# A table's copies moved to ScalarE and its zeros to GpSimd; in a chain of two pairs, ScalarE in program order and the pairs one turn apart

## The chip, the cores and the metric

The kernel runs on one core of one Trainium2 chip. The time is device microseconds (us) of one execution; lower is better. A core has five instruction queues that run beside each other: TensorE (PE, with its weight loads shown as PEld), VectorE (DVE), ScalarE (ACT), GpSimd (POOL) and SyncE (SP), which issues most of the DMAs. ScalarE and GpSimd issue some DMAs too. Instructions of different queues wait for each other through semaphores.

## The reference, cut to what matters

Four layers follow each other on an activation `x` of 4 batches x 512 tokens x 128 channels, all float32. Each layer is a half-weighted feed-forward part, an attention-like part, and the same feed-forward part again. The parts that this change touches are these:

```python
# layer 0: a mixture of 8 experts (top 1), then attention with a relative-position table
x = x + 0.5 * L0_ffn(layernorm(x), ...)            # "first mixture"
x = x + L0_attn(layernorm(x), ..., rel_pos_emb)    # the table: 16 heads, causal
...
# the end of layer 1, layer 2, and the start of layer 3
x = x + 0.5 * L1_ffn(layernorm(x), ...)   # sigmoid scores, top 2 of 8, swiglu experts, a shared one
x = x + 0.5 * L2_ffn(layernorm(x), ...)   # top 2 of 8 by logits; y += gate_e * (x @ w_in_e.T @ w_out_e.T)
x = x + L2_attn(layernorm(x), ...)        # sigmoid gates, then h = 0.9 h + 0.1 g over the tokens
x = x + 0.5 * L2_ffn(layernorm(x), ...)
x = x + 0.5 * L3_ffn(layernorm(x), ...)   # "third mixture": top 2 of 8 experts with a capacity
```

The relative-position table of layer 0 is `rel_pos_emb` summed over the 8 channels of a head, and it enters the attention scores as a bias that depends on the distance of the two tokens.

## The kernel before, in words

A batch of 512 tokens is a tile `xs[b]` of 128 partitions x 4 token blocks x 128 channels, and it stays in SBUF from the first to the last part. The kernel is written with a planner that decides the order of each queue at compile time: among the instructions that it takes to be ready it prefers those that stand earlier in the program. Inside `tc.manual_schedule(engines={...})` the named queues keep the order of the program instead.

**The table.** `prep_table` (L1012 and on) builds the bias table, 128 partitions x 16 heads x 512. A short row for each head is written to DRAM (`tab_rows`). Eight DMAs on ScalarE's queue (L1037), for two heads each, read it back so that each partition is shifted by one (`rev`, 128x512). TensorE turns each block over with the matrix `flip` into a PSUM bank (L1042), VectorE copies the bank into the last 256 columns of the table (L1043), and VectorE sets the other 256 columns of all heads to zero (L1044). This generator is run out at the end of a block in which all four compute queues keep the order of the program, after the routing of the first mixture (`f00.tokens`) and ahead of its experts (`f00.experts`). The same block ends with the transposed biases `b1T` (L570, a VectorE copy at L571) and with zeros that GpSimd writes for the attention (`padded_values`, L585). The experts themselves are not in the block, so the planner may put their instructions between those of the block. Per expert TensorE transposes the tokens (L466), multiplies with `w1` (L490), ScalarE and VectorE evict with the bias `b1T` (L494, L495), TensorE multiplies with `w2` (L526), and GpSimd scatters the rows to DRAM (L512). `rev` comes out of the pool tag `"raw"` of five buffers, which the zeros `z` of the mixture and `b1r` use as well.

**The chain.** From the second feed-forward part of layer 1 to the routing of the third mixture the batches go in two pairs, `[0, 1]` and `[2, 3]`, each a generator `behind(pool, bs)`. It runs `l1_ffn`, `l2_ffn`, `l2_attn`, `l2_ffn` and `f30.tokens`. A `yield` ends a step, and `skewed(gens, lag)` runs one step of each pair per turn, pair 0 ahead, with pair 1 starting `lag` turns later. What a pair does in its steps, counted from 0 in each part:

- `l1_ffn`: 12 steps for pair 0, whose norms and gates were made during the attention; 17 for pair 1, which first makes norms (`norms`, L168 to L187: VectorE statistics, GpSimd `rstd` and `off`, then half of the tiles on ScalarE at L182 and half on VectorE at L186), transposes (L195, copies at L1124), scores and gates. The gates go to DRAM and come back spread over partitions (`cb`, L1242). For each of five chunks: two matmuls (L1218, L1219), a sigmoid (L1222), two VectorE products (L1223, L1224), a GpSimd product with `cb` (L1265), and the down matmuls (L1253).
- `l2_ffn`: 9 steps. Steps 0 to 2 are norms and transposes, 3 the logits (L1133) and the first products (L1419), 4 the routing on VectorE and two sigmoids (L1434, L1436), 5 to 8 are the four gated rounds: 16 VectorE instructions each (L1450) that add a gated product to `x`.
- `l2_attn`: 9 steps: 3 of norms, then for each batch projection and two sigmoids (L1471, L1473), the scan over the tokens on VectorE (L1478), and the output.
- `f30.tokens`: norms (all on ScalarE), logits, the exponential (L348), routing on VectorE, and 16 scatters per pair by GpSimd's indirect DMA (L416). Pair 0 takes two steps of it per turn and one scatter per step.

In this stage GpSimd keeps the order of the program; the other queues are ordered by the planner. Before it stands the attention of layer 1, behind it the experts of the third mixture, whose first load waits for the last scatter.

Of the kernel before, what the change touches and what calls it, by code (L numbers as in the profile page):

```python
# [9 lines left out]
FP = mybir.dt.float32  # L10
# [7 lines left out]
P = 128  # L18
D = 128
NB, S = 4, 512  # L20
# [4 lines left out]
NH = 16  # L25
# [16 lines left out]
def kernel(ctx: ExitStack, tc: tile.TileContext, a: dict, out: bass.AP):  # L42
    nc = tc.nc
# [5 lines left out]
    stage = ctx.enter_context(tc.tile_pool(name="stage", bufs=5))  # L49
# [3 lines left out]
    def const(shape, name, dtype=FP):  # L53
        return cpool.tile(shape, dtype, name=name, tag=name)

    def bank(name):
        return psum.tile([P, 512], FP, name=name, tag="bank", bufs=8)
# [19 lines left out]
    flip = const([P, P], "flip")  # L77
# [934 lines left out]
    def prep_table(pool):  # L1012


        rel = stage.tile([P, D], FP, name="rel", tag="rel", bufs=1)
        nc.sync.dma_start(rel, a["L0_attn_rel_pos_emb"][P - 1 : 2 * P - 1, :])
        yield

        table = pool.tile([P, NH, S], FP, name="table", tag="table", bufs=1)
        tab = stage.tile([P, NH], FP, name="tab", tag="tab", bufs=1)  # L1020
        nc.vector.tensor_reduce(tab, rel.rearrange("p (h d) -> p h d", d=HD), AX.X, ALU.add)
        ps = bank("tabT")
        nc.tensor.matmul(ps[:NH, :P], tab, flip, start=True, stop=True)
        last = stage.tile([NH, 1], FP, name="tab_last", tag="tab_last", bufs=1)
        nc.vector.tensor_copy(last, ps[:NH, 0:1])
        row = stage.tile([NH, 3 * P], FP, name="tab_row", tag="tab_row", bufs=1)
        nc.vector.memset(row[:, :P], 0.0)
        nc.vector.tensor_scalar(row[:, P : 2 * P], ps[:NH, :P], last, None, ALU.subtract)
        nc.vector.memset(row[:, 2 * P :], NEG)
        rows = dram.tile([NH, 3 * P], FP, name="tab_rows", tag="tab_rows")  # L1030
        nc.sync.dma_start(rows, row)
        yield

        for h in range(0, NH, 2):

            rev = stage.tile([P, 2, 2 * P], FP, name=f"rev{h}", tag="raw")
            nc.scalar.dma_start(  # L1037
                rev,
                bass.AP(tensor=rows.tensor, offset=rows.offset + h * 3 * P, ap=[[1, P], [3 * P, 2], [1, 2 * P]]),
            )  # L1040
            ps = bank(f"turned{h}")
            nc.tensor.matmul(ps, flip, rev.rearrange("p h s -> p (h s)"), start=True, stop=True)  # L1042
            nc.vector.tensor_copy(table[:, h : h + 2, S - 2 * P :], ps.rearrange("p (h s) -> p h s", h=2))  # L1043
        nc.vector.memset(table[:, :, : S - 2 * P], 0.0)  # L1044
        l0["table"] = table
        yield

# [523 lines left out]
    def whole(parts):  # L1571
        for _ in parts:
            pass

    def skewed(gens, lag):

        live = {i: g for i, g in enumerate(gens)}
        r = 0
        while live:
            for i in list(live):  # L1580
                if r >= i * lag and next(live[i], "end") == "end":
                    del live[i]
            r += 1
            yield
# [19 lines left out]
    pairs = [[b, b + 1] for b in range(0, NB, 2)]  # L1604
    gate0T = wpool.tile([D, E], FP, name="gate0T", tag="gate0T")
    ps = bank("gate0T")
    nc.tensor.transpose(ps[:, :E], gate0, ident[:E, :E])
    nc.vector.tensor_copy(gate0T, ps[:, :E])
    with tc.tile_pool(name="tables", bufs=1) as tables:
        f00 = Mixture("f00", CAP0, 1)  # L1610
        f00.zeroed(stage, "raw", 5)
        made = prep_table(tables)
        next(made)
        whole(f00.empty())
# [31 lines left out]
    with tc.tile_pool(name="weights12", bufs=1) as mid:  # L1646
# [39 lines left out]
        def behind(pool, bs):  # L1686
            yield from l1_ffn(pool, 1, bs, early if bs[0] == 0 else None)
            yield from l2_ffn(pool, 0, bs)
            yield from l2_attn(pool, bs)
            yield from l2_ffn(pool, 1, bs)  # L1690
            if bs[0] == 0:

                parts = f30.tokens(bs, l3["gate"], "scalar", pool, apart=True)
                while next(parts, "end") != "end" and next(parts, "end") != "end":
                    yield
            else:
                yield from skewed([f30.tokens([b], l3["gate"], "scalar", pool) for b in bs], 4)

        with tc.tile_pool(name="chain", bufs=2) as pool:
            decay = pool.tile([P, S], FP, name="decay", tag="decay", bufs=1)  # L1700
            nc.gpsimd.memset(decay, 0.9)
            with tc.manual_schedule(engines={mybir.EngineType.Pool}):
                whole(skewed([behind(pool, bs) for bs in pairs], 4))
        pools["w"] = wpool
    prep_l3_attn()
    with tc.tile_pool(name="padded", bufs=1) as pool:
# [52 lines left out]
```

## Time and profile before

| what | value |
| --- | --- |
| median of 3 runs | 1507.65 us (1504.37 to 1510.55) |
| the profiled execution, its own time | 1506.45 us |
| its span, first to last instruction | 1504.7 us |
| PE busy | 1258.4 us (84%) |
| DVE busy | 893.8 us (59%) |
| ACT busy | 685.7 us (46%) |
| POOL busy | 691.0 us (46%) |
| mean granted TensorE clock | 0.908 |

The profile is of one execution, and its times count from the span's start. Busy shares are averages over stages with different limits, so the views below are read stage by stage. In a row of the timeline the columns are start, duration, engine, line, operation, output<-input, the shape and how many instructions were merged; the bracket gives the idle time of the engine ahead of it and what ended it. In a row of the stretches each engine has its busy time and, in brackets, its number of instructions; the granted TensorE clock and the DMA share follow. The chain that ended last follows the work back from the last instruction to what released each step.

### The profile page before, as it was taken

The page shows a single profiled execution, that of the slowest core. Times are in us where ns is not written, and L with a number is a line of the kernel's source. Part 1 is how long each engine was busy: PE and PEld are TensorE (multiplying, and loading weights), DVE is VectorE, ACT ScalarE, POOL GpSimd, SP SyncE. Part 2 cuts the span into 40 slices and gives each one's busy share as a digit, 9 for nine tenths or more (in the row PEclk, how much of TensorE's full clock was granted, in tenths as well). Part 3 has the DMA queues.
Part 4 walks back from the last instruction along what each step waited for, and adds up shares of the span by engine and source line. Part 5 has one row for each costly group of instructions (what it writes and reads, how often), then busy time and mean ns, then how long its engine had stood idle before and what let it go on. Part 6 is the DMA issues. An engine that isn't in the chain of part 4 may idle for free.

```text
span 1504.7 us, 28029 instructions
## 1 busy us (share of the span) xinstructions
PE 1258.4 (84%) x10133; PEld 787.1 (52%) x10133; DVE 893.8 (59%) x3105; ACT 685.7 (46%) x1438; POOL 691.0 (46%) x810
## 2 busy tenths in 40 slices
PE   4788999995979989998999766439599999998394
PEld 4465666674756656676655334227453334333273
DVE  5326766663345657777467766634277787773243
ACT  2135867871443367776621213104245555564041
POOL 5346767872433678876432112554502224212343
PEclk9998999996999999999999776759799999999597
DMA  9420240002413884241130000032105000000223
GB/s 254 114 60 12 80 171 13 9 5 74 137 52 61 228 259 136 93 141 31 32 80 3 1 1 0 29 92 79 56 8 184 9 11 5 15 2 15 78 82 108
DMA packets 100657, 106.15 MB, mean 71 GB/s; under 512 B 9084, under 2 KB 73832, under 8 KB 100520
## 3 DMA queue, kind: packets, MB, share of 16 engines
q1 hardware_dynamic: 89576, 88.01, 20.3%
q0 software_dynamic: 6656, 13.22, 2.5%
q10 hardware_dynamic: 4288, 3.15, 0.8%
q8 instruction: 80, 1.31, 0.3%
q14 instruction: 57, 0.47, 0.1%
HBM read 62.49 MB, written 41.85 MB: 69 GB/s over the span
## 4 chain that ended last, share of the span: by engine, by line
PE 63%; DVE 13%; POOL 9%; issue 7%; DMA 6%; ACT 2%; SPq 0%; POOLq 0%; DVEq 0%; ACTq 0%
PE s_a L621 13%; PE t_a L666 9%; PE o_f L526 5%; PE h_f L490 5%; PE acc_a L688 5%; PE acc_a L826 4%; DVE x L1450 3%; PE t_a L621 3%; PE y_f L1419 2%; POOL disp_f L416 2%; PE ot_a L845 2%; POOL res_f L512 2%; PE gu_f L1218 1%; PE gu_f L1219 1%; PE T_f L195 1%
## 5 line engine op out<-in xcount | busy, mean ns | idle before, releaser
L653 POOL TENSOR_SCALAR sc_a<-sc_a,top_a 128x128 f32<-128x128 f32 (+3 forms) x256 | 275.8, 1092 | 88.0 <-DVE top_a L638 53.8
L621 PE MATMUL s_a<-k_a,q_a 32*128 32x512 f32 (+3 forms) x1536 | 265.1, 539 | 6.0 <-DVE top_a L642 4.8
L710 DVE TENSOR_REDUCE low<-s_a 128x1 f32<-128x512 f32 x256 | 163.0, 684 | 42.8 <-PE t_a L621 31.0
L730 ACT ACTIVATE w_a<-t_a 128x512 f32<-128x512 f32 x240 | 131.6, 596 | 107.1 <-PE t_a L621 69.2
L666 PE MATMUL t_a<-ident,sc_a 128*128 128x128 f32 x1280 | 171.6, 279 | 7.4 <-DVE top_a L642 6.7
L512 POOL DMA_INDIRECT res_f<-y_f,back_f x112 | 106.6, 952 | 140.1 <-ACT y_f L511 92.3
L666 PEld LDWEIGHTS t_a<-ident,sc_a 128*128 128x128 f32 x1280 | 142.8, 143 | 42.6 <-issue 15.8
L621 PE MATMUL t_a<-ql_a,k_a 32*128 32x512 f32 x480 | 157.9, 640 | 0.4 <-DVE low L710 0.3
L655 ACT ACTIVATE sc_a<-sc_a,top_a 128x128 f32<-128x128 f32 (+3 forms) x256 | 134.7, 575 | 16.1 <-DVE top_a L642 15.6
L621 PEld LDWEIGHTS s_a<-k_a,q_a 32*128 32x128 f32 x1536 | 94.7, 186 | 74.5 <-issue 39.0
L675 ACT ACTIVATE w_a<-t_a 128x256 f32<-128x256 f32 (+2 forms) x192 | 94.3, 526 | 70.4 <-PE t_a L666 70.0
L416 POOL DMA_INDIRECT disp_f<-n_f,to_f x96 | 94.8, 988 | 51.5 <-issue 37.2
L526 PE MATMUL o_f<-w_l,h_f 128*128 128x128 f32 (+1 forms) x896 | 111.9, 280 | 3.6 <-ACT h_f L494 3.6
L526 PEld LDWEIGHTS o_f<-w_l,h_f 128*128 128x128 f32 (+1 forms) x896 | 103.9, 186 | 12.6 <-ACT h_f L494 5.6
L490 PE MATMUL h_f<-dT_f,w_l 128*128 128x320 f32 (+1 forms) x256 | 106.6, 555 | 2.8 <-ACT dT_f L468 2.8
L172 POOL TENSOR_SCALAR rs_f<-mv_f 128x4 f32<-128x4 f32 (+1 forms) x23 | 5.3, 231 | 203.4 <-DVE mv_f L169 202.9
L688 PE MATMUL acc_a<-w_a,vpad 128*32 128x128 f32 x2560 | 97.7, 278 | 0.6 <-ACT w_a L675 0.6
L677 ACT COPY w_a<-t_a 128x256 f32<-128x256 f32 (+2 forms) x192 | 93.5, 526 | 5.7 <-PE t_a L666 5.7
L642 DVE CUSTOM_DVE_ANT_0 sc_a<-s_a,table 128x128 f32<-128x128 f32 (+3 forms) x128 | 62.3, 487 | 46.8 <-PE s_a L621 35.2
L642 DVE CUSTOM_DVE_ANT_0 sc_a<-s_a,future 128x128 f32<-128x128 f32 (+3 forms) x128 | 62.4, 487 | 46.3 <-PE s_a L621 39.5
L511 ACT ACTIVATE y_f<-o_f,d_f 128x128 f32<-128x128 f32 (+1 forms) x112 | 38.9, 394 | 105.2 <-DVE o_f L506 93.5
L826 PE MATMUL acc_a<-w_a,vpad 128*32 128x256 f32 x1024 | 82.5, 391 | 2.7 <-ACT w_a L730 2.3
(338 smaller groups left out, 2200.6 us busy)
## 6 DMA issues: line engine op xcount, KB each, us to landing
fac_a<-fac_a_sb SPq DMA_DIRECT2D x36, 256.0 KB
disp_f<-zeros_f SPq DMA_DIRECT2D x4, 2080.0 KB
d_f<-disp_f SPq DMA_DIRECT2D x32, 260.0 KB
w_l<-in_L_ffn_w_dram SPq DMA_DIRECT2D x16, 512.0 KB
cb_f<-rows_f SPq DMA_DIRECT2D x16, 512.0 KB
q_a<-fac_a SPq DMA_DIRECT2D x32, 256.0 KB
k_a<-fac_a SPq DMA_DIRECT2D x32, 256.0 KB
r_f<-res_f SPq DMA_DIRECT2D x16, 256.0 KB
```

What stands on the lines that cost most here:

```text
L416: nc.gpsimd.indirect_dma_start(out=self.to[c][i0 + t][:, :], out_offset=bass.IndirectOffsetOnAxis(ap=to[:, c, t : t + 1], axis=0), in_=ns[ ...
L490: nc.tensor.matmul(ps[u][:, :cap], w1[:, e, (c + u) * P : (c + u + 1) * P], dT, start=True, stop=True)
L512: nc.gpsimd.indirect_dma_start(out=self.back[e * per + s][:, :], out_offset=bass.IndirectOffsetOnAxis(ap=back[:m, s : s + 1], axis=0), in_ ...
L526: nc.tensor.matmul(po[:m, s, :], h[:, c, s * P : s * P + m], w2[:, e, c, :], start=(c == 0), stop=(c == NC - 1),)
L621: nc.tensor.matmul(ps[:, n0:n1], q[r : r + SLOT, i * P : (i + 1) * P], k[r : r + SLOT, n0:n1], start=True, stop=True)
L653: nc.gpsimd.tensor_scalar(sc, sc, top, None, ALU.subtract)
L655: nc.scalar.activation(sc, sc, AF.Exp, bias=top, scale=-1.0)
L666: nc.tensor.transpose(ps[:, x * n + j * P : x * n + (j + 1) * P], st["sc", u, i, r0 + x][:, j * P : (j + 1) * P], ident,)
L688: nc.tensor.matmul(st["acc", u][r * SLOT : (r + 1) * SLOT, i * P : (i + 1) * P], vpads[b % 2][:, j, g * 4 + r, :], st["w", u, i, r][:, j * ...
L710: nc.vector.tensor_reduce(st["low", u][:, i, c : c + 1], ps, AX.X, ALU.max, negate=True)
L730: nc.scalar.activation(w, ps, AF.Exp)
L826: nc.tensor.matmul(acc[r * SLOT : (r + 1) * SLOT, n0:n1], vpads[b % 2][:, j, g * 4 + r, :], st["w", u, j, r, half] if ("w", u, j, r, half) ...
```

## The change

In `prep_table` the eight copies go from VectorE to ScalarE, and the zeros from VectorE to GpSimd. ScalarE's queue also issues the DMAs of `rev`; with its copies now on the same queue, the first three DMAs are issued ahead and each of the other five behind a copy. In the chain ScalarE keeps the order of the program too, and pair 1 starts one turn behind pair 0 in place of four.

```diff
-        for h in range(0, NH, 2):
-            rev = stage.tile([P, 2, 2 * P], FP, name=f"rev{h}", tag="raw")
+        revs = {}
+        def fetch(h):
+            revs[h] = stage.tile([P, 2, 2 * P], FP, name=f"rev{h}", tag="raw")
             nc.scalar.dma_start(
-                rev,
+                revs[h],
                 bass.AP(tensor=rows.tensor, offset=rows.offset + h * 3 * P, ap=[[1, P], [3 * P, 2], [1, 2 * P]]),
             )
+        for h in range(0, 6, 2):
+            fetch(h)
+        for h in range(0, NH, 2):
             ps = bank(f"turned{h}")
-            nc.tensor.matmul(ps, flip, rev.rearrange("p h s -> p (h s)"), start=True, stop=True)
-            nc.vector.tensor_copy(table[:, h : h + 2, S - 2 * P :], ps.rearrange("p (h s) -> p h s", h=2))
-        nc.vector.memset(table[:, :, : S - 2 * P], 0.0)
+            nc.tensor.matmul(ps, flip, revs[h].rearrange("p h s -> p (h s)"), start=True, stop=True)
+            nc.scalar.copy(table[:, h : h + 2, S - 2 * P :], ps.rearrange("p (h s) -> p h s", h=2))
+            if h + 6 < NH:
+                fetch(h + 6)
+        nc.gpsimd.memset(table[:, :, : S - 2 * P], 0.0)
...
-            with tc.manual_schedule(engines={mybir.EngineType.Pool}):
-                whole(skewed([behind(pool, bs) for bs in pairs], 4))
+            with tc.manual_schedule(engines={mybir.EngineType.Pool, mybir.EngineType.Activation}):
+                whole(skewed([behind(pool, bs) for bs in pairs], 1))
```

## The prediction

> **What bounds the kernel now.** I read the page's busy shares and its chain of waits, then the chain in order of time around the two edits, then the timeline, and last the busy time by stretch.
>
> ```profile
> span 1504.7 us, 28029 instructions
> PE 63%; DVE 13%; POOL 9%; issue 7%; DMA 6%; ACT 2%; SPq 0%; POOLq 0%; DVEq 0%; ACTq 0%
> ```
>
> TensorE is on the chain for 63%, so most of the kernel is set by matmuls that the change does not touch. What counts is whether the two edited places lie on the chain; both do.
>
> In front of the first mixture (timeline):
>
> ```profile
> 51.73 4.27 DVE L1043 COPY table<-turned 128x512 f32<-128x512 f32 x7
> ...
> 52.62 0.61 PE L466 MATMUL dT_f<-ident,d_f 128*128 128x128 f32 x3 [2.38 <-DMA raw_ow0T<-in_L_attn_proj_w_dram]
> ...
> 56.80 3.47 DVE L1044 MEMSET table<- 128x4096 f32 x1 [0.80 <-issue]
> ...
> 60.19 0.13 DVE L571 COPY b1T_l<-b_l 128x32 f32<-128x32 f32 x1
> 60.35 0.94 ACT L494 ACTIVATE h_f<-h_f,b1T_l 128x320 f32<-128x320 f32 x2 [1.49 <-DVE b1T_l L571]
> ...
> 60.94 1.44 PE L526 MATMUL o_f<-w_l,h_f 128*128 128x128 f32 x5 [2.53 <-ACT h_f L494]
> ```
>
> Seven of the table's copies and the zeros hold VectorE from 51.73 to 60.27. The copy of `b1T` stands behind them, and the first eviction of the experts (L494) waits 1.49 us for it. TensorE's transposes waited at 52.6 until the first of these copies gave a bank back. The chain in order of time has these copies (4.19) and the zeros (3.47).
>
> In the chain of the pairs, busy time by stretch; I put the borders at the first and last gated instructions (L1450) of a pair:
>
> ```profile
> 803.50:828.80 25.30, 23.38 (x85) 12.66 (x83) 23.53 (x76) 2.98 (x5) 5.08 (x4) 1.00 0.00 0
> 828.80:850.50 21.70, 15.85 (x57) 9.26 (x58) 13.17 (x62) 7.58 (x17) 7.48 (x10) 0.69 0.00 1
> 850.50:871.90 21.40, 14.01 (x33) 6.44 (x31) 19.96 (x73) 0.69 (x1) 0.00 (x0) 0.84 0.00 0
> 871.90:890.40 18.50, 13.21 (x39) 8.60 (x40) 9.18 (x53) 5.52 (x14) 7.43 (x10) 0.54 0.00 0
> 890.40:917.50 27.10, 18.55 (x50) 8.96 (x49) 24.96 (x85) 2.75 (x4) 0.00 (x0) 0.94 0.00 1
> 917.50:941.00 23.50, 16.73 (x57) 12.46 (x58) 11.20 (x63) 10.04 (x21) 8.10 (x18) 0.50 0.01 3
> 941.00:960.70 19.70, 12.24 (x28) 5.02 (x26) 17.05 (x65) 0.00 (x0) 10.02 (x11) 0.93 0.12 38
> 960.70:1001.80 41.10, 11.25 (x44) 9.12 (x44) 11.44 (x72) 6.47 (x14) 24.87 (x39) 0.50 0.10 33
> ```
>
> In 803–829, 851–872, 890–917 and 941–961 one pair's gated rounds fill VectorE (20.0 of 21.4, 25.0 of 27.1). In 829–851, 872–890 and 917–941 nobody gates: 63.7 us, of which VectorE works 33.6, at granted clocks of 0.69, 0.54 and 0.50. There both pairs stand in their norms at once, because the lag of 4 and the five more steps of pair 1's first part put pair 1 nine turns behind, exactly one part (9 steps). Each then goes through statistics, GpSimd's power (1.67), ScalarE, transposes, logits and routing with nothing to cover it.
>
> Two rows show what a fixed order costs and what a free one does; the last rows are the end of the stage:
>
> ```profile
> 787.54 2.50 POOL L1265 TENSOR_TENSOR h_f<-h_f,cb_f 128x512 f32<-128x512 f32 x2 [5.42 <-DMA cb_f<-rows_f]
> ...
> 790.13 0.24 POOL L172 TENSOR_SCALAR rs_f<-mv_f 128x8 f32<-128x8 f32 x1
> ...
> 972.91 1.28 ACT L348 ACT_TABLE_LOAD   x1
> ...
> 974.46 0.21 DVE L239 SCALAR_TENSOR_TENSOR rest_r<-masks_f,pr_f 128x32 f32<-128x32 f32 x1 [4.38 <-ACT pr_f L348]
> ...
> 999.21 0.95 POOL L416 DMA_INDIRECT disp_f<-n_f,to_f  x1 [0.30 <-DMA disp_f<-n_f,to_f]
> ...
> 1001.92 1.49 SPq L447 DMA_DIRECT2D d_f<-disp_f  x3
> ```
>
> GpSimd, in program order, took pair 0's `rs` at 790.13 although its statistics were done at 786.1: two products ahead of it waited for `cb` until 787.54. And ScalarE, in the planner's order, put three norms of batch 3 and a table load ahead of batch 2's exponential; VectorE waited 4.38 us. The scatters end at 1000.2, and the third mixture's load follows.
>
> **The change part by part: the table.** Removed from VectorE: 7 copies and the zeros, 51.73 to 60.27, 8.5 us. ScalarE is idle from 28.7 to 53.4, and its copy of 128x512 out of PSUM takes 0.58 (L321) against VectorE's 0.68 (L1043): eight are 4.6 us, hidden as far as data is there (all of it, if not). But the DMAs change. Before, all eight issues went out between 34.21 and 45.16 and the last block was turned at 50.07. Now each later DMA waits for a copy. The first block took 4.1 us from issue (34.21) to matmul (38.33); with 0.9 for the matmuls, 0.6 for the copy, 0.4 for the issue, a round is 6.0 us and serves three blocks. The first copies end at 40.6, 42.2 and 43.6, so blocks 6 and 7 are turned by about 52.1 and 53.6. Then transposes 53.9, dT's copy, `w1` from 55.2 (53.87 before), 4.1 us for it, second transposes 0.6: `w2` begins at 60.0 where it began at 60.94, and does not stall for its second half (0.6). That is -1.5; with a landing in 2.9 us, as for `r_f` at 110.33, it is -4; with a landing of 6 us it is +3. I take -2.
>
> GpSimd's zeros: the row of its 128x2048 memset is 1.82, so 128x4096 is 3.6. [...] SP's queue is not passed by anything here; its load of `d_f` (47.04) stays.
>
> **The change part by part: the chain.** Pair 1 is now six turns behind pair 0, so the norms of one fall beside the gated rounds of the other. ScalarE's 54 us in 745 to 1002 bind nothing by their sum, only by their order. I walk through the turns with rows of the trace: chunk of `l1_ffn` 2.6 us on PE, GpSimd product 1.27, gated round 4.2, norm to first gated instruction 14.7 (VectorE 2.1, `rs` and power 2.0, `off` 0.6, ScalarE 1.65, last transpose and copies 1.7, logits 1.9, routing 3.2, sigmoids and gates 1.6), a batch of `l2_attn` 3.3 on VectorE.
>
> Layer 1. On GpSimd pair 1's norm now stands behind one product of pair 0, not four: 754.7 in place of 759.1. On ScalarE these norms (turn 2) stand ahead of pair 0's sigmoids of chunks 3 and 4, which go from 753.5 and 755.2 to 759 and 762; queued behind them are two products on VectorE and on GpSimd each. Pair 0's first batch ends at 766.8 (762.1). Pair 1's gates are done at about 769 (776.7) and its `cb` is there at 779.8 (787.5), since both of SP's transfers move with the gates. But pair 1's first product is now ahead of three of pair 0's second batch on GpSimd, and waits for that `cb`: from 779.8 seven products of 1.27 follow, and pair 0 ends at 789 (783.5). Its norm then waits for nothing: gating begins at 805.5 (803.5). Pair 1's first part ends near 809.5 (828.2).
>
> Then the gated rounds. Pair 0 gates 17 us, with 2.4 of pair 1's last products and 3.2 of its norm on VectorE: 828. Pair 0's statistics 2.1 and pair 1's routing 3.8: pair 1 gates from 834 (850.5), with 7.7 of pair 0's attention: 858.5 (871.9). Now pair 1's attention norm, then pair 0's norm on GpSimd behind it, and on ScalarE pair 0's norm behind pair 1's first sigmoids (870.6): pair 0 gates from 883 (890.4). 17 and 3.2: 903.5 (917.5). Pair 0's last norm stands on ScalarE (8 instructions, 3.2) ahead of pair 1's two sigmoids, which costs 4.5: pair 1 gates from 914 (941), and with 5 of pair 0's routing it ends at 936 (960.7): -25.
>
> The tail. Before, 12 of pair 0's scatters went ahead of batch 2's norm on GpSimd and 4 behind; now 6 ahead and 10 behind. A scatter is 0.96 and 0.30 to the next. From the end of gating: statistics and norm 4, ten scatters 12.6, batch 3's norm and small writes 3.5, sixteen scatters 20.2, counts 0.7: 41 us against 39.5: +1.5. Batch 2's rows are ready 16 us after the gating, so they don't wait.
>
> Table loads. The row is 1.28, three in this stage before, after the first one: exponential (927.75), sigmoid (931.47), exponential (972.91). With six turns pair 1's last sigmoids come one turn ahead of pair 0's first exponential, so one is left. [...]
>
> Sum: -2, -25, +1.5. The walk takes VectorE as full in the gated stretches, where it was 92%, and TensorE at full clock: 5 us back. That is -20.5. The profiled execution is 1506.45 (span 1504.7 and 1.75 around it), so 1486; its 1.2 to the median of 1507.65 gives 1487.
>
> **The rivals.**
> A: the walk holds, 1487 (1475 to 1499).
> B: more, 1470. If ScalarE's fixed order costs none of the 18 us that I charged (4.7, 5.5 on GpSimd, 4.5, and 3 to 4 at 870) and the clock stays up where it was 0.50 to 0.69. For: 64 us of poor cover. Against: the order is fixed, and the row at 790.13 shows that it costs.
> C: no change, 1503. The stretches close, but the two pairs then ask for the eight PSUM banks at once: two rounds of products hold all of them, and transposes and logits wait. Only the front and a few us stay. For: products already wait for banks that VectorE gives back (2.3 us in the stage). Against: small so far.
> D: slower, 1518. GpSimd's program order, in one place: pair 1's first product. If pair 1's gates are not earlier (VectorE busy with pair 0), its `cb` comes at 787.5 as before; the seven products end at 796.4, pair 0's norm is taken at 798.5 (790.1), +8.4, and if the planner then finds no better cover all later stretches shift; with the tail +4 and the front -2 that is +10. It decides from a `cb` later than about 785 together with stretches that stay open.
> E: the pin on ScalarE does nothing, since the planner's order was the program's already; then only the lag acts. That lies within A and B.
>
> **How the numbers follow.** A 0.50, B 0.14, C 0.17, D 0.16, and 0.03 for worse. About 0.5% (7.5 us) is what a measurement of this kernel can tell from no change. Faster (under 1500): A but for its edge, B, and a little of C: 0.68. Same: 0.15. Slower (over 1515): 0.17. The range leaves out part of D and the far end of B: 1465 to 1515.
>
> **What would show it.** VectorE is at `b1T` before 53; the last `turned` matmul ends at 52 to 55. No stretch of over 12 us without L1450 between the first and the last, but for one of about 20 after pair 1's first gating. The last L1450 ends 20 to 30 us sooner after the start of `l1_ffn` (745.5 to 960.7 is 215 before). One table load for exponentials. Wrong would be: GpSimd idle over 8 us at L1265 on `cb`, ScalarE idle over 5 us on `off` with sigmoids ready behind, or a tail from the last L1450 to the last scatter of over 45 us.

## The result, and the profile after

The change made the kernel faster: 1494.46 us (median of 14 runs) against 1505.76 for the kernel before, a ratio of 0.9923 with a 95% interval of 0.9907 to 0.9940. That is 11.3 us where 20.5 were predicted. A second set of timed runs of the same two kernels gave 0.9912 (0.9892 to 0.9933). The profiled execution took 1497.54 us with a span of 1495.8.

The head of the page, and its chain of waits by engine:

```profile
span 1495.8 us, 28015 instructions
...
PE 64%; DVE 12%; POOL 7%; issue 7%; DMA 6%; ACT 2%; SPq 0%; POOLq 0%; ACTq 0%; DVEq 0%
```

The shares hardly moved; what moved is local. The span is cut here at three places that both traces show: the start of the last projection matmul of layer 1's attention (called L866 below), where the chain of the pairs starts; the end of the last gated instruction (L1450 before, L1458 after); and the first matmul of the third mixture (L490).

| stretch | before | after | difference |
| --- | --- | --- | --- |
| start to L866 | 745.5 | 743.8 | -1.7 |
| L866 to the last gated instruction | 215.2 | 206.3 | -8.9 |
| from there to the third mixture's first matmul | 47.7 | 47.9 | +0.2 |
| the rest | 496.3 | 497.8 | +1.5 |

The front, in the timeline of the changed kernel:

```profile
53.87 1.10 PE L1048 MATMUL turned<-rev,flip 128*128 128x512 f32 x2 [2.46 <-DMA rev<-tab_rows]
...
55.18 0.19 DVE L571 COPY b1T_l<-b_l 128x32 f32<-128x32 f32 x1 [0.39 <-PE b_l L570]
...
56.35 4.64 PE L490 MATMUL h_f<-dT_f,w_l 128*128 128x320 f32 x8 [0.64 <-ACT dT_f L468]
...
57.83 0.53 ACT L494 ACTIVATE h_f<-h_f,b1T_l 128x320 f32<-128x320 f32 x1 [1.53 <-PE h_f L490]
...
61.65 2.45 PE L526 MATMUL o_f<-w_l,h_f 128*128 128x128 f32 x16
```

`b1T` is no longer what the first eviction waits for (L494 now waits for the matmul), and the second matmuls no longer stall. But the last block is turned 4.9 us later than before (54.97 for 50.07), TensorE stands still for 2.46 us in front of it, and the eight matmuls of `w1` behind take 4.64 us.

Two lines of the kernel before belong beside this. They show why seven of the copies came so late there, and what `w1` took:

```profile
50.11 0.16 DVE L472 SCALAR_TENSOR_TENSOR lost_f<-d_f,astray 128x3 f32<-128x3 f32 x1 [8.98 <-DMA d_f<-disp_f]
...
53.87 4.11 PE L490 MATMUL h_f<-dT_f,w_l 128*128 128x320 f32 x8 [0.64 <-ACT dT_f L468]
```

The banks were turned from 38.33 on, but in VectorE's queue seven of the copies stood behind instructions of the first expert that waited for DMAs, the first of them until 50.11. On ScalarE they have no such neighbour, and the first three run at 41.67, 43.38 and 45.08; what the change waits for instead is the DMA of the last block.

The chain of the pairs, busy time by stretch with the borders at the first and last gated instruction of a pair (start:end and length, then PE, PEld, DVE, ACT, POOL busy, the granted clock, DMA share, GB/s):

```profile
810.70:831.70 21.00, 17.78 (x76) 10.20 (x75) 20.61 (x81) 2.75 (x6) 3.63 (x5) 1.00 0.00 1
831.70:841.40 9.70, 4.40 (x14) 2.26 (x13) 7.41 (x35) 2.83 (x8) 4.94 (x6) 0.79 0.00 0
841.40:863.50 22.10, 17.98 (x40) 8.21 (x39) 19.93 (x71) 2.83 (x5) 0.00 (x0) 0.86 0.00 0
863.50:898.40 34.90, 21.20 (x65) 13.53 (x65) 20.12 (x74) 8.42 (x18) 8.77 (x10) 0.71 0.00 1
898.40:918.00 19.60, 17.59 (x55) 9.51 (x56) 19.30 (x78) 2.75 (x6) 2.36 (x4) 0.86 0.00 0
918.00:929.50 11.50, 10.05 (x34) 5.46 (x34) 5.53 (x36) 5.94 (x14) 3.13 (x8) 0.80 0.00 0
```

Before, three stretches without gating made 63.7 us. Now they are 9.7, 34.9 and 11.5, together 56.1: two were halved, and the middle one, 18.5 before, has grown to 34.9. VectorE works 20.1 of it. The timeline at its end shows what it waits for:

```profile
886.71 6.28 PE L1427 MATMUL y_f<-m,nT_f 128*128 128x512 f32 x8
...
889.31 0.16 DVE L1440 TENSOR_TENSOR apart_f<-mx,mx 128x8 f32<-128x8 f32 x1
...
892.83 1.88 PE L1477 MATMUL proj_a<-nT_a,win 128*128 128x512 f32 x4
...
893.89 0.69 ACT L1479 ACTIVATE gate_a<-proj_a,bin2T 128x512 f32<-128x512 f32 x1 [13.97 <-PE proj_a L1477]
894.75 0.69 ACT L1481 ACTIVATE hid_a<-proj_a,bin2T 128x512 f32<-128x512 f32 x1 [0.17 <-PE proj_a L1477]
895.33 0.20 ACT L1442 ACTIVATE g_f<-apart_f 128x8 f32<-128x8 f32 x1
...
898.45 1.39 DVE L1458 SCALAR_TENSOR_TENSOR x<-y_f,gates_f,x 128x128 f32<-128x128 f32 x5
```

Pair 0's routing is done at 889.47 (`apart`). Its gating sigmoid (L1442) needs nothing else, yet runs at 895.33, 5.9 us later. ScalarE had been idle for 13.97 us: in its fixed order the sigmoids of pair 1's second attention batch (L1479, L1481) stand ahead, and these wait for a projection (L1477) that TensorE takes behind pair 0's eight products (L1427). The same happens at pair 0's first gating: `apart` is done at 804.88, the sigmoid runs at 807.67, behind a chunk sigmoid of pair 1 (L1230) for which ScalarE sat idle for 7.18 us. At pair 1's last gating the sigmoid stands behind pair 0's eight norms and two copies, and VectorE waits 4.56 us for it.

```profile
807.18 0.60 ACT L1230 ACTIVATE h_f<-gu_f 128x512 f32<-128x512 f32 x1 [7.18 <-PE gu_f L1226]
807.67 0.20 ACT L1442 ACTIVATE g_f<-apart_f 128x8 f32<-128x8 f32 x1
...
927.35 0.23 DVE L1448 SCALAR_TENSOR_TENSOR mask<-mask,g_f 128x64 f32<-128x64 f32 x1 [4.56 <-ACT g_f L1442]
```

The end of the stage on GpSimd:

```profile
944.95 0.96 POOL L416 DMA_INDIRECT disp_f<-n_f,to_f  x1 [0.30 <-issue]
951.00 0.22 POOL L172 TENSOR_SCALAR rs_f<-mv_f 128x4 f32<-128x4 f32 x1 [5.10 <-DVE mv_f L169]
...
988.65 0.96 POOL L416 DMA_INDIRECT disp_f<-n_f,to_f  x1 [0.30 <-DMA disp_f<-n_f,to_f]
```

From the last gated instruction (950.1) to the last scatter's end it is 39.5 us, as before.

### The profile page after: what moved, and what is told of

The parts are those of the page before. It is cut to its first block, busy times and chain, and to the rows that moved or that the text cites. A ratio compares the mean times of both kernels' runs of the same rounds, so it can differ in the third digit from the quotient of the medians.

```text
span 1495.8 us, 28015 instructions
## 1 busy us (share of the span) xinstructions
PE 1260.0 (84%) x10133; PEld 784.3 (52%) x10133; DVE 885.6 (59%) x3096; ACT 688.5 (46%) x1444; POOL 697.2 (47%) x811
## 3 DMA queue, kind: packets, MB, share of 16 engines
q8 instruction: 80, 1.31, 0.4%
## 4 chain that ended last, share of the span: by engine, by line
PE 64%; DVE 12%; POOL 7%; issue 7%; DMA 6%; ACT 2%; SPq 0%; POOLq 0%; ACTq 0%; DVEq 0%
PE s_a L621 13%; PE t_a L666 9%; PE h_f L490 5%; PE acc_a L688 5%; PE o_f L526 5%; PE acc_a L826 5%; DVE x L1458 3%; PE t_a L621 3%; PE y_f L1427 2%; POOL disp_f L416 2%; PE ot_a L845 2%; PE o_f L1261 2%; POOL res_f L512 2%; PE gu_f L1226 2%; PE gu_f L1227 1%
## 5 line engine op out<-in xcount | busy, mean ns | idle before, releaser
L490 PE MATMUL h_f<-dT_f,w_l 128*128 128x320 f32 (+1 forms) x256 | 107.0, 557 | 2.8 <-ACT dT_f L468 2.8
L642 DVE CUSTOM_DVE_ANT_0 sc_a<-s_a,table 128x128 f32<-128x128 f32 (+3 forms) x128 | 62.3, 487 | 45.3 <-PE s_a L621 34.9
```

The costliest lines, as they stand in the source:

```text
L490: nc.tensor.matmul(ps[u][:, :cap], w1[:, e, (c + u) * P : (c + u + 1) * P], dT, start=True, stop=True)
```

## The experiments

Three groups of four kernels were timed, each group beside the kernel before on a chip of its own. The kernel before took 1508.9, 1496.5 and 1506.6 us there, so the groups are compared through their ratios, and single times only within a group. Traces differ between chips too: the chain of the whole change takes 206.3 us in its first profile and 203.0 in the second group's. Two medians give the sign of a difference; intervals are given where they decide.

### First group: the parts of the change

**The table's part alone.** In the chain, both edits are undone:

```diff
-            with tc.manual_schedule(engines={mybir.EngineType.Pool, mybir.EngineType.Activation}):
-                whole(skewed([behind(pool, bs) for bs in pairs], 1))
+            with tc.manual_schedule(engines={mybir.EngineType.Pool}):
+                whole(skewed([behind(pool, bs) for bs in pairs], 4))
```

> The table's part alone: copies on ScalarE and zeros on GpSimd in front of the first mixture, the chain as before (ScalarE by the planner, lag 4). Theory: what the edit saves in front of the first mixture, 1.7 us in the trace of the change (proj_a of layer 1 ends at 743.8 in place of 745.5), is handed through: 1.5 to 2 us faster than before (ratio 0.999), the chain from 744 to the last gated round as long as before, about 215. Rival: the saving is swallowed at the next wait for a DMA, and the time is that of before; or the front is worth more than the trace shows and carries a good part of the 11 us.

1502.89 us, ratio 0.9953 (0.9938 to 0.9968): 7.1 us faster by the ratio, not 1.7. The chain starts at 738.9, 6.6 us sooner than before, and is as long as before (214.1). In its timeline the front differs from that of the whole change, with the same instructions in the same order:

```profile
53.48 1.10 PE L1048 MATMUL turned<-rev,flip 128*128 128x512 f32 x2 [1.59 <-DMA rev<-tab_rows]
...
55.95 2.42 PE L490 MATMUL h_f<-dT_f,w_l 128*128 128x320 f32 x8 [0.64 <-ACT dT_f L468]
...
58.72 2.05 PE L526 MATMUL o_f<-w_l,h_f 128*128 128x128 f32 x16
```

The matmuls of `w1` take 2.42 us here and took 4.64 in the profile of the change. The granted clock is the difference, first the change and then this kernel:

```profile
56.00:58.00 2.00, 1.65 (x3) 1.18 (x4) 0.00 (x0) 0.47 (x2) 0.00 (x0) 0.50 0.85 255
```

```profile
56.00:58.00 2.00, 2.00 (x8) 1.45 (x9) 0.55 (x1) 0.65 (x2) 0.00 (x0) 1.00 0.68 197
```

The expectation failed because it took the front's gain from one profile. That execution happened to run its first expert at half clock. Three of this group's kernels have the changed front: all ran it at a clock of 1.00, and their second mixture starts at 365.8 to 366.6, against 373.0 and 373.9 in the two profiles with the old front. The old front fell to half clock both times, and twice each time: for `w1`, and again for the second matmuls after TensorE had waited for the eviction behind `b1T`, 2.53 us in the kernel before and 2.71 in the chain's part alone (the kernel before; columns as above, the granted clock third from the end):

```profile
54.00:56.00 2.00, 2.00 (x5) 1.22 (x6) 2.00 (x4) 0.00 (x0) 0.00 (x0) 0.52 0.30 85
...
58.00:60.00 2.00, 0.40 (x3) 0.13 (x1) 2.00 (x1) 0.42 (x1) 0.00 (x0) 1.00 0.00 0
...
62.00:64.00 2.00, 2.00 (x11) 2.00 (x11) 0.00 (x0) 0.00 (x0) 0.00 (x0) 0.50 0.00 0
```

The clock in front of the experts accounts for a part of the gain only. The second expert's first matmul starts at 60.6 here and at 64.4 before, 3.8 us sooner. The rest of the 6.6 us comes by the end of layer 0's attention. The kernel before has another half-clock stretch of 3.4 us there (0.50 from 214.5 to 217.9), but the profile of the change has one as well (212.7 to 216.1). Where this part of the gain comes from is not shown.

**The chain's part alone.** The kernel before with ScalarE in program order and lag 1:

```diff
-            with tc.manual_schedule(engines={mybir.EngineType.Pool}):
-                whole(skewed([behind(pool, bs) for bs in pairs], 4))
+            with tc.manual_schedule(engines={mybir.EngineType.Pool, mybir.EngineType.Activation}):
+                whole(skewed([behind(pool, bs) for bs in pairs], 1))
```

> The chain's part alone: ScalarE in program order and lag 1, the table's part as before. Theory: 9 to 10 us faster than before (ratio 0.9937), the stage from its start to the last gated instruction 206 us in place of 215. Rival: the front carries it, and this is under 5 us faster.

1499.72 us, ratio 0.9941 (0.9919 to 0.9962): 8.9 us faster. From L866 to the last gated instruction it is 206.5 us, and the middle stretch is 34.9 us with ScalarE idle for the same 13.97 us. The two parts alone make 7.1 and 8.9; together they gave 11.3 and 13.2 in the two sets. The intervals of the parts are wide enough (2.3 and 3.2 us to each side) for that, and the front's clock varies between executions, so no loss between the parts can be read from it.

**The lag without ScalarE's program order.** Only the lag is kept in the chain:

```diff
-            with tc.manual_schedule(engines={mybir.EngineType.Pool, mybir.EngineType.Activation}):
+            with tc.manual_schedule(engines={mybir.EngineType.Pool}):
                 whole(skewed([behind(pool, bs) for bs in pairs], 1))
```

> The whole change but for ScalarE's program order in the chain: lag 1, ScalarE by the planner. The planner puts the gating sigmoids of pair 0 ahead of pair 1's last chunk sigmoids and, in the second feed-forward part, ahead of the attention sigmoids of pair 1's second batch. Theory (the lag makes the gain, the program order takes part of it back, where gating sigmoids stand behind sigmoids that wait for matmuls: 2.8 us at 805, 5.9 us at 889): faster than the whole change by 4 to 8 us, 1487 to 1490. Rival (the program order is what makes the gain, by keeping norms and the exponential's table load out of the way): slower than the change by 4 us or more, 1499 and up.

1491.02 us, ratio 0.9881 (0.9860 to 0.9903): 17.9 us faster than before. The lag makes the gain: without it, with the same front and the same order by the planner, it was 7.1 us. The program order takes some 5 to 6 us of it back (0.9881 against 0.9923 and 0.9912; the interval of the second overlaps this one's). The chain takes 202.7 us, against 206.5 with the program order on the same chip. Pair 0's first gating starts 60.4 us after L866 in place of 67.0, and the middle stretch is shorter by 7.6:

```profile
854.00:881.30 27.30, 17.19 (x57) 11.82 (x58) 17.42 (x70) 6.92 (x16) 8.77 (x10) 0.66 0.00 1
881.30:908.00 26.70, 22.00 (x68) 11.18 (x67) 22.41 (x83) 4.12 (x8) 2.35 (x4) 0.90 0.00 0
```

The second row shows why the chain gained only 3.6: the next gated rounds take 26.7 us, where they took 19.6 in the change. Some of pair 1's attention, which VectorE did in the wait before, now falls into the rounds.

**ScalarE's program order without the lag.** Only the order is kept:

```diff
             with tc.manual_schedule(engines={mybir.EngineType.Pool, mybir.EngineType.Activation}):
-                whole(skewed([behind(pool, bs) for bs in pairs], 1))
+                whole(skewed([behind(pool, bs) for bs in pairs], 4))
```

> The whole change but for the lag: ScalarE in program order, lag 4 as before. Theory: the order hardly changes (the planner's order differs from the program's in a handful of places), so this is within 3 us of the table's part alone, 1501 to 1506. Rival: the program order makes the gain, and this is 5 us or more faster than the table's part alone.

1499.51 us, ratio 0.9946 (0.9925 to 0.9967), as good as the table's part alone (0.9953). So the order by itself is worth nothing that these runs can tell. In its trace it does one thing well. The planner had put batch 3's norms (L182) and a table load ahead of batch 2's exponential, for which VectorE waited 4.4 us. In program order the norms stand behind:

```profile
956.90 1.28 ACT L348 ACT_TABLE_LOAD   x1
...
959.30 0.23 ACT L348 ACTIVATE pr_f<-pr_f 128x32 f32<-128x32 f32 x1 [1.12 <-DVE pr_f L346]
...
961.62 1.65 ACT L182 ACTIVATE n_f<-x,off_f,rstd_f 128x128 f32<-128x128 f32 x4 [2.09 <-POOL off_f L177]
```

From the last gated instruction to the third mixture it is 43.4 us in this profile and 47.9 with the table's part alone. With lag 1 this is not seen again (47.9 with the program order, 47.8 without).

### Second group: the wait of the gating sigmoids, the front, the lag

**The change once more**, as the base of this group, nothing edited.

> The change itself once more, on the chip of the three others of this call. Both theories of the chain: 0.992, about 11 us faster than before, 206 us from the start of the chain to the last gated instruction. For the front: if TensorE's clock in front of the first expert is a matter of the execution and not of the program, the eight first matmuls with w1 may take 2.4 us here (as in the three runs with the table's edit) or 4.6 us (as in the profile of the change); if it belongs to the program, 4.6.

1483.80 us, ratio 0.9912 (0.9892 to 0.9933). L866 at 740.8, the chain 203.0 us, the middle stretch 34.7. TensorE did the eight matmuls of `w1` in 4.06 us, with a clock of 0.53 from 56 to 58, behind an idle time of 1.31 us. Both profiles of this program have the drop, so by itself this run does not tell program from execution. What speaks for the execution is that the three kernels above run the same instructions in the same order up to there, at full clock.

**Routing and gating sigmoids a step earlier.** The turn saved is put back behind them, so the pairs stay six turns apart:

```diff
         products(0, 0)
-        yield
         m1, v1 = route(pool, lg, G, "0")
...
         nc.scalar.activation(g2, apart, AF.Sigmoid, scale=-1.0)
         yield
+        yield
```

> The change with the routing and its two gating sigmoids a step earlier in the program (the step behind is left empty, so the pairs stay aligned): in ScalarE's fixed order the gating sigmoids then stand ahead of pair 1's last chunk sigmoid but one, of the attention sigmoids of pair 1's second batch, and of pair 0's token copies; nothing else of that queue moves. Theory (they stand behind sigmoids that wait for matmuls: 2.8 us at 805, 5.9 us at 889, 4.6 us at 922): gating of pair 0 starts 3 us and 6 to 10 us earlier after the start of the chain, the last gated instruction comes 4 to 9 us earlier (197 to 202 us after the start, in place of 206), and so does the time. Rival (the order only trades one wait for another, the sigmoids of pair 1 now wait behind the routing): within 2 us of the change.

1475.46 us, ratio 0.9852 (0.9837 to 0.9868), 8.3 us faster than the change in this group; the intervals do not touch. The wait is gone where it was predicted to go:

```profile
878.17 0.21 ACT L1441 ACTIVATE g_f<-apart_f 128x8 f32<-128x8 f32 x1 [9.65 <-DVE apart_f L1439]
```

```profile
880.97 1.45 PE L1477 MATMUL proj_a<-nT_a,win 128*128 128x512 f32 x3
```

The gating sigmoid (now L1441) runs as soon as `apart` is there and waits for nothing else, although pair 1's projection still comes late, at 880.97. Pair 0's gating starts 62.7 us after L866 (65.4 in this group's run of the change) the first time and 141.5 (151.5) the second time. The stretches behind give most of that back again:

```profile
852.00:879.50 27.50, 16.92 (x57) 12.02 (x58) 17.85 (x71) 7.15 (x16) 8.77 (x10) 0.63 0.00 1
879.50:905.10 25.60, 20.91 (x68) 11.18 (x67) 22.47 (x83) 4.12 (x8) 2.35 (x4) 0.93 0.00 0
905.10:913.70 8.60, 5.23 (x14) 2.11 (x12) 4.71 (x29) 3.97 (x12) 3.12 (x8) 0.80 0.00 0
913.70:939.10 25.40, 17.30 (x44) 9.74 (x44) 21.49 (x94) 1.91 (x3) 6.61 (x10) 0.70 0.05 17
```

The gated rounds are 25.6 and 25.4 us here and 19.6 and 20.6 in the profile of the change. Of these 10.8 us, some 4.5 are work: VectorE does the other pair's attention and routing inside them. Another 4.6 are two waits in VectorE's own queue, where an instruction of the other pair stands ahead of gated ones and waits for an attention sigmoid and for the routing's logits:

```profile
883.61 0.75 DVE L1483 SCALAR_TENSOR_TENSOR hid_a<-proj_a,bin2T,hid_a 128x512 f32<-128x512 f32 x1 [1.91 <-ACT hid_a L1481]
...
917.25 0.22 DVE L344 TENSOR_REDUCE mx_f<-lg_f 128x8 f32<-128x64 f32 x1 [2.69 <-PE lg_f L330]
```

The third wait that the expectation named, ahead of pair 1's last gating, is still there: 3.54 us in place of 4.56. The last gated instruction comes 201.1 us after L866, which is within what was expected, but only 1.9 us sooner than in this group's run of the change (203.0). The span is 5.4 us shorter: 1.9 in the chain, 2.8 in front of L866, which the edit does not touch (the clock was full in front of its first expert), and 0.7 behind. The profiled execution is the slowest of its four (1478.31 us), 2.9 above their median, and this makes up the difference to the 8.3 us of the medians. So the traces show 2 us of gain in the chain; what the sigmoids have to do with the rest is not shown.

**Five DMAs of `rev` ahead in place of three:**

```diff
-        for h in range(0, 6, 2):
+        for h in range(0, 10, 2):
             fetch(h)
...
-            if h + 6 < NH:
-                fetch(h + 6)
+            if h + 10 < NH:
+                fetch(h + 10)
```

> The change with five DMAs of rev issued ahead in place of three, and the other three behind copies. Theory (the fourth and fifth DMA waited in the change behind the first copies, issued at 41.7 and 43.4, though their buffers were free from about 38.3): last block turned at 50 to 52 in place of 54.4, the experts' first matmul then held by another load at about 53, so 1 to 3 us earlier in front, and a shorter idle time of TensorE in front of the first expert, so that its clock is full there. In all 1 to 3 us faster than the change where the clock was full, up to 6 where it was not. Rival (the front is bound by the DMAs' bandwidth, which is busy for 0.66 to 0.8): no change.

1479.44 us, ratio 0.9890 (0.9868 to 0.9913), 4.4 us under the change's median, with intervals that overlap. In the trace the step did what was expected of it:

```profile
48.01 3.16 PE L1048 MATMUL turned<-rev,flip 128*128 128x512 f32 x6 [1.52 <-DMA rev<-tab_rows]
51.10 0.24 PE L570 MATMUL b_l<-ident,b1r_l 32*128 32x32 f32 x1
51.56 0.61 PE L466 MATMUL dT_f<-ident,d_f 128*128 128x128 f32 x3 [0.22 <-DMA d_f<-disp_f]
52.81 2.42 PE L490 MATMUL h_f<-dT_f,w_l 128*128 128x320 f32 x8 [0.64 <-ACT dT_f L468]
```

The last block is turned at 51.2 in place of 54.8 in this group's run of the change, the experts start 3.4 us sooner, and L866 is 6.3 us sooner (734.5). The chain is that of the change (203.3).

**Lag 2, ScalarE by the planner:**

```diff
-            with tc.manual_schedule(engines={mybir.EngineType.Pool, mybir.EngineType.Activation}):
-                whole(skewed([behind(pool, bs) for bs in pairs], 1))
+            with tc.manual_schedule(engines={mybir.EngineType.Pool}):
+                whole(skewed([behind(pool, bs) for bs in pairs], 2))
```

> Lag 2 and ScalarE by the planner; the table's part as in the change. Pair 1 is seven turns behind pair 0 instead of six. Theory (the gain is from the norms of one pair standing beside the gated rounds of the other, four of nine steps): with seven turns the gated rounds overlap the other's norms by one step less, so 2 to 5 us slower than lag 1 by the planner (which was 6 us faster than the change): 1492 to 1496. Rival (any shift from nine turns does as well, or a shift of seven fits better because the first parts no longer compete): as fast as lag 1 by the planner or faster, 1490 or less.

1486.71 us, ratio 0.9935 (0.9910 to 0.9960), some 8 us worse than lag 1 by the planner (0.9881), where 2 to 5 were expected. The chain is 212.2 us. The stretches without gating are 12.0, 25.5 and this one:

```profile
906.40:929.50 23.10, 18.55 (x57) 12.64 (x58) 8.67 (x55) 9.10 (x19) 3.96 (x12) 0.51 0.00 0
```

It has the look of the stretches of before: VectorE busy for 8.7 of 23.1 us, the clock at 0.51. So the seventh turn puts the norms side by side again.

### Third group: both edits that helped, and what is left of the rest

**Both edits together:** sigmoids a step earlier and five DMAs ahead, ScalarE in program order.

> The change with both edits that helped: routing and gating sigmoids a step earlier, and five DMAs of rev ahead. Theory: the two places are apart, so what they gave adds up: 0.9852 with the sigmoids alone, 0.002 to 0.004 more for the front: 0.981 to 0.983, 25 to 28 us faster than before. Rival: the stages in between absorb it, or what the timed runs gave to the sigmoids alone (more than its trace showed) was partly the front's clock: 0.985.

1487.64 us, ratio 0.9872 (0.9852 to 0.9893): not better than the sigmoids alone (0.9852). The theory of adding up is not borne out. In its profile the last block was turned at 49.9 and the clock still fell:

```profile
51.35 0.61 PE L466 MATMUL dT_f<-ident,d_f 128*128 128x128 f32 x3 [1.31 <-DMA d_f<-disp_f]
52.60 3.88 PE L490 MATMUL h_f<-dT_f,w_l 128*128 128x320 f32 x8 [0.64 <-ACT dT_f L468]
```

The three kernels below have the same order on TensorE in the front and ran it at a clock of 1.00, so the earlier DMAs do not make the clock safe. Their second mixture starts at 362.3 to 363.0, 3 us ahead of the first group's, but the timed runs do not show it on top of the sigmoids. The chain is 200.5 us, some 3 less than with the five DMAs alone.

**The same with ScalarE by the planner** (`engines={mybir.EngineType.Pool}`).

> The same with ScalarE by the planner in the chain. Theory (the program order cost only through the place of the gating sigmoids, and that is mended): within 3 us of the one before. Rival (the program order also costs elsewhere, for example through norms of one pair ahead of sigmoids of the other): 4 us or more faster.

1488.50 us, ratio 0.9881 (0.9861 to 0.9901), the same as with the program order. With the sigmoids a step earlier, the order has no cost left that can be measured.

**The same in program order with lag 0:**

```diff
-                whole(skewed([behind(pool, bs) for bs in pairs], 1))
+                whole(skewed([behind(pool, bs) for bs in pairs], 0))
```

> The first of this call (program order, sigmoids a step earlier, five DMAs ahead) with lag 0: pair 1 five turns behind pair 0 in place of six. Theory (what counts is that one pair's four gated rounds fall on the other's five steps of norm and routing): five turns do that as well as six, within 4 us of it either way. Rival (in layer 1 pair 1's norm then stands ahead of all of pair 0's products on GpSimd, and its chunks compete with pair 0's on TensorE): 5 us or more slower.

1486.84 us, ratio 0.9867 (0.9846 to 0.9888), the same as lag 1. The chain is 199.1 us, the shortest of all, but from its end to the third mixture it is 50.7 us in place of 47.5, so little of that is left.

**The same with the zeros back on VectorE:**

```diff
-        nc.gpsimd.memset(table[:, :, : S - 2 * P], 0.0)
+        nc.vector.memset(table[:, :, : S - 2 * P], 0.0)
```

> The first of this call with the table's zeros back on VectorE, the copies staying on ScalarE. Theory (once the copies are gone VectorE is idle while the last blocks are turned, and the zeros wait for nothing): b1T still comes ahead of the first eviction, and the time is the same within 2 us; the copies alone carry the front's gain. Rival (3.5 us of zeros push b1T or the experts' slots back): 2 to 4 us slower.

1488.33 us, ratio 0.9879 (0.9859 to 0.9899), no difference. `b1T` comes at 53.24, ahead of the eviction at 53.68. Where the zeros run doesn't matter once the copies are gone. That the zeros' move by itself would give nothing is not shown; it was not run alone.

The best versions are thus at 0.985 to 0.988 of the kernel before, 0.004 to 0.007 under the change. Among them these runs cannot choose.

## Why the prediction was right, and where its sizes were off

The direction and the mechanism were right: the two parts act in two places, and the lag, by setting one pair's norms beside the other's gated rounds, carries the chain's gain. The sum was not: -20.5 against -11.3. Two terms were mis-sized, in opposite directions, the chain by far the most. That the time still came within 7.5 us of the 1487 is in part luck: the front gave more than its term, for a reason that the prediction did not have.

**The front, -2.** The profile of the change has -1.7 and seemed to confirm it, the last block at 54.97 for 53.6. The timed run of this part alone has -7.1. The working took `w1` at its price of before, 4.1 us. That was a price at half clock; at full clock the same matmuls take 2.42. (The row of the transposes at 52.62 names a DMA that they do not read. The prediction's reading, a bank that the first copy gave back, fits both profiles with the old front: the copy ends at 52.41 and 54.08, the transposes start at 52.62 and 54.28.) With VectorE out of the way TensorE no longer stands still behind `w1`, and in four of the seven profiles with this front the clock stays up throughout. This explains 3.8 us of the 6.6 that the trace gained; the rest, in layer 0's attention, stays open. The sum has nothing for GpSimd's zeros. They took 3.54 us (from 44.33 on), against the 3.6 estimated and the 3.47 of VectorE before. Behind them and the attention's pads GpSimd still stood idle for 13.43 us ahead of its first scatter (65.28), so they hid, and the run with them on VectorE shows no difference.

**The chain, -25.** It gave -8.9. Measured from L866, the walk against what came:

| step | predicted | the change | sigmoids a step earlier |
| --- | --- | --- | --- |
| pair 0 gates, first time | 60.0 | 67.0 | 62.7 |
| pair 1 gates, first time | 88.5 | 97.7 | 93.8 |
| pair 0 gates, second time | 137.5 | 154.7 | 141.5 |
| pair 1 gates, second time | 168.5 | 185.7 | 175.7 |
| last gated instruction | 190.5 | 206.3 | 201.1 |

The first step is 7.0 late. Pair 1's gates were done 4 us later than walked, so `cb` released GpSimd's products at 782.0 and pair 0's first part ended 4.4 us late (at 791.65). The gating sigmoid's wait behind a chunk sigmoid adds 2.8. The third step loses another 8: the sigmoid's wait of 5.9, with VectorE taking up pair 1's attention ahead of the gates at its end. The other steps are within about 2 us. The prediction had charged 18 us for fixed orders, but in other places: 4.7 on chunk sigmoids behind norms, 5.5 on GpSimd behind `cb`, 3 to 4 at 870, 4.5 ahead of pair 1's last gating. The last was there (VectorE waited 4.56 us). The two that it missed are of one kind: it looked for ScalarE idle on a norm's `off`, and ScalarE was idle on matmuls of the other pair, with a ready sigmoid behind. The run with the sigmoids a step earlier takes these two waits away, and the first four steps come within 3 to 7 us of the walk.

**The tail, +1.5, and the return of 5.** The tail is 39.5 us as before, so its +1.5 was 0. The 5 us taken off for VectorE not being full and for the clock was of the right kind and too small. With the sigmoids a step earlier, the rounds that were to take 20.5 and 22 us take 25.6 and 25.4: VectorE is not full in them, since it waits 1.91 and 2.69 us on the other pair. The half clock also has a price in one place: the eight products at 886.71 took 6.28 us at a granted clock of 0.58, those at 802.60 took 3.68 at 1.00, and pair 1's projection stood behind them.

**The rivals.** A (the walk holds) has the result inside its own range of 1475 to 1499, 7.5 us above its middle. B (the fixed order costs nothing) promised too much: even with the planner's order or the sigmoids earlier it is 18 to 21 us, not 36. C (the PSUM banks) is not seen: the longest wait of a gated instruction for its product is 1.2 us, and the products waited 2.6 us in all for banks that VectorE gives back, where it was 2.3 before. D (GpSimd's queue behind `cb`) did not come about; `cb` was there at 782, before the 785 from which it decides. E (the pin does nothing) is answered on both sides: at lag 4 it does nothing that can be timed, at lag 1 it costs some 5 to 6 us.

Of the signs named in advance, the main one failed: the last gated instruction came 8.9 us sooner after the start of the chain, not 20 to 30. `b1T` at 55.18 came later than the 53 expected, because its matmul stood behind the last `turned`; the last `turned` matmul (54.97), the single table load for the exponentials and the tail held. The load (927.43, 1.28 us) starts where the last sigmoid ends (927.42), and the exponential behind it waits another 0.52 us for VectorE, so it holds nothing up. The 12 us limit for stretches without gating broke in one place as foreseen, with 34.9 us in place of about 20. One of the signs of being wrong appeared as well:

```profile
755.86 1.65 ACT L182 ACTIVATE n_f<-x,off_f,rstd_f 128x128 f32<-128x128 f32 x4 [6.17 <-POOL off_f L177]
...
757.41 0.57 ACT L1230 ACTIVATE h_f<-gu_f 128x512 f32<-128x512 f32 x1
```

ScalarE was idle for 6.17 us on `off`, and the chunk sigmoid behind had its products since 752.5. This is the wait for which the prediction charged 4.7 us. GpSimd's idle times on `cb` (6.81 us for pair 0's, 5.05 for pair 1's) and the tail stayed under their limits.

## What to carry to other kernels

When two streams of work share a queue in a fixed order, look for short instructions that release a long stage (here a sigmoid of 0.2 us ahead of 64 gated instructions) and ask what each instruction ahead of them in that queue waits for; putting the short one a step earlier in the program gave about what dropping the order gave. A profile is one execution: a term that depends on the granted clock needs its price at both clocks, and timed runs of that part alone. And a wait that is removed pays only as far as the work behind it can move up: here some 10 us won at one step shrank to 2 by the end of the trace's chain. VectorE had used the wait for work that it then had to do inside the next rounds, and there it waited for the other pair, in a queue of its own that two streams share.

## What was not expected of the hardware

In front of the first expert the granted TensorE clock differs between executions with one and the same instruction order. After idle times of 2.38 to 2.60 us ahead of the transposes or the last turned block (the two profiles with the old front, and the first of the change) the eight matmuls behind ran at about half clock each time, 3.9 to 4.6 us. After 1.3 us they did in two profiles (4.06 and 3.88) and took 2.42 in the others, up to an idle time of 1.59. With lag 2 the clock fell too, from 51.8 to 55.2 behind an idle time of 1.26, and was back just ahead of `w1`. So an idle time of about 1.3 us can go either way. The half clocks lasted 3.4 us (56.1 to 59.5 in the second profile of the change, 53.4 to 56.8 with both edits) or twice that (55.7 to 62.5 in the first). Between 44 us and the first expert TensorE was never idle for longer than 2.6 us at a time. What decides between the two clocks is not shown.

The DMAs that stand behind a copy in ScalarE's queue did not wait for the copy's end: in the profile of the change all five are issued within 0.06 us of the copy's start, the first at 41.73 for a copy from 41.67 to 42.26. The prediction's 0.6 us for the copy in each round of DMAs was therefore too much, without bearing on the result.
